# Layer 0 of a four-layer graph network: gathers of node rows held until an earlier relu has run

## The chip, the cores and the metric

The kernel runs on one core of a Trainium2 chip. The metric is the device time of one execution in microseconds (us); the number given for a kernel is the median of its runs.

## The reference, cut to what matters

A graph has 3,125 nodes with 128 features and 100,000 edges, sorted by destination. Four layers follow each other, each with a residual and a layer norm. The change is in layer 0, an attention over each node's incoming edges:

```python
hP1 = h @ P1; hP2 = h @ P2; zP3 = z @ P3             # h: nodes, z: 500 relations
pre_edge = hP1[dst] + hP2[src] + zP3[edge_type]
logit_edge = _leaky(pre_edge) @ y_w                  # 8 heads
# softmax over the edges of each destination (and the node itself) gives alpha
t_edge = hWh[src] + zWz[edge_type]
agg = segment_sum(alpha * t, dst)
out = _leaky(agg + residual_weight * h)
```

Layer 1 is a mean over neighbours with two dense layers, layers 2 and 3 are attentions with other scores. They aren't touched.

## The kernel before

**Tiles and slots.** Nodes are ordered by degree and cut into 25 tiles of 128; a node lies on a partition. Tile `t` has `CAP[t]` slots (57 down to 21): slot `s` holds the `s`-th incoming edge of each of the 128 nodes. There are 821 slots in all. `runs(t)` cuts the slots into chunks of at most `W = 8` and groups them into runs of two or three chunks; it yields 114 chunks.

**Rows.** Before the loop, a table `h_tab` of one row per node (264 floats: the part for the logits, the part for the messages, 8 more for the logits) and a table `z_tab` per relation are written to HBM. For each slot one indirect DMA (`gather`, line 102, issued by POOL) brings the row of the source node onto each of the 128 partitions of `hs`. `hs` has 8 buffers, each for one chunk.

**Two kinds of chunk.** In a "gathered" chunk (`gathered`, L842) the rows of the relation are gathered as well, into `zs` (2 buffers), and DVE adds them (L849). In a "multiplied" chunk (`multiplied`, L860), 77 of the 114, the relation's part comes by matrix products: `rb` is loaded on SP's queue (L866), DVE makes one-hots `oh` (L871), PE forms `zps` (L880), ACT copies it to `zT` (L882). In both, groups of four slots follow: PE collects the argument in `pre` (L822, L884, and L856 or L886, which read `hs`), ACT takes the relu into `low` (`logits`, L829), PE multiplies it into `lg` (L831). There are 215 such groups.

**After a run.** `masked`, `weights` and `faded` make the softmax of the run; `spread` (L915) weighs the message part of `hs` and adds it up. The `spread`s of a run are put off and issued during the next one (`owed`, `pay_some`); with the last of them a buffer of `hs` comes free. `close(t, ...)` (L941) ends a tile: `y` (L988), its layer norm `x1` (L758), which POOL writes to HBM (L991, through L105). Between chunks, `counts` (L574) makes a count matrix for layer 1, piece by piece, with one-hots on DVE and products on PE.

**Order.** Each engine runs its instructions in a fixed order. A planner sets it from the order of the program, its own costs and the dependencies; it inserts the semaphores. POOL's queue in layer 0 holds the gathers of `hs` and `zs`, a memset and a load of `x` for the next tile (`own`, L797 to L799), and the store of `x1`. A gather of `hs` may be issued once the buffer that it takes has been read for the last time.

Of the kernel before, what the change touches and what calls it, by code (L numbers as in the profile page):

```python
# [8 lines left out]
F32 = mybir.dt.float32  # L9
# [3 lines left out]
AF = mybir.ActivationFunctionType  # L13
# [7 lines left out]
NT = 25  # L21
# [30 lines left out]
CW = 512  # L52
NCW = -(-NP // CW)
AHEAD = 600


def chunks(t):
# [11 lines left out]
def runs(t):  # L69

    n = (3 * CAP[t] + 2 * W) // (4 * W)
    k, part = CAP[t] // W, CAP[t] % W
    rest = [part] * (part > 0) + [W] * (k - n)
    k = n + len(rest)
    cs, s = [], 0
    for i in range(k):
        mult = (i + 1) * n // k > i * n // k
        w = W if mult else rest.pop(0)  # L80
        cs.append((s, w, mult))
        s += w
    m = -(-k // 3)
    return [cs[i * k // m:(i + 1) * k // m] for i in range(m)]
# [3 lines left out]
def tile_gnn(ctx, tc, a, out):  # L88
    nc = tc.nc
    V, A, G, T = nc.vector, nc.scalar, nc.gpsimd, nc.tensor  # L90
# [7 lines left out]
    def indirect(ap):  # L98
        return bass.IndirectOffsetOnAxis(ap=ap, axis=0)

    def gather(dst, table, idx, **kw):
        return G.indirect_dma_start(out=dst, out_offset=None, in_=table, in_offset=indirect(idx), **kw)  # L102
# [395 lines left out]
    with tc.tile_pool(name="srcp", bufs=1) as sp, tc.tile_pool(name="srcq", bufs=2, space=PSUM) as ps:  # L498
# [28 lines left out]
        for o in range(0, NS, P):  # L527
            n = min(P, NS - o)
# [248 lines left out]
    with tc.tile_pool(name="l0", bufs=2) as wp, tc.tile_pool(name="l0s", bufs=1) as sp, \  # L777
# [5 lines left out]
        V.memset(m, LOW)  # L783
        l = sp.tile([P, NT, H], F32, name="l")
        V.memset(l, 0.0)
        nosum = sp.tile([P, D + R], F32, name="nosum")
        V.memset(nosum, 0.0)
        sums_at = sums_tab.rearrange("(t p) d -> t p d", p=P)
# [34 lines left out]
                         stop=False)  # L823
            return pre

        def logits(pre, k, lg_ps):

            low = wp.tile([P, 4, P], F32, name="low")
            A.activation(low[:, :k], pre[:, :k], AF.Relu)  # L829
            for s in range(k):  # L830
                T.matmul(lg_ps[:, s, :], low[:, s, :], yw8, start=True, stop=True)  # L831

        def halved(v, n, last=None):

            while n > 2:
                k = n // 2
                V.tensor_add(v[:, :k], v[:, :k], v[:, n - k:n])
                n -= k
            if n == 2:
                V.tensor_add(v[:, 0] if last is None else last, v[:, 0], v[:, 1])  # L840

        def gathered(hq, idx, rl, n, za, lg_ps):  # L842

            hs = wp.tile([P, W, HC], F32, name="hs", bufs=8)
            zs = wp.tile([P, W, HC + R], F32, name="zs")
            for s in range(n):
                gather(hs[:, s, :], h_tab, idx(s))
                gather(zs[:, s, :], z_tab, rl[:, s:s + 1])
            V.tensor_add(hs[:, :n], hs[:, :n], zs[:, :n, :HC])  # L849
            halved(zs[:, :, HC:], n)  # L850
            V.tensor_add(za, za, zs[:, 0, HC:])  # L851
            for s0 in range(0, n, 4):
                k = min(4, n - s0)
                pre = argument(hq, k)
                for s in range(k):
                    T.matmul(pre[:, s, :], hs[:, s0 + s, :D], ident, start=False, stop=(s == k - 1))  # L856
                logits(pre, k, lg_ps[:, s0:s0 + k])
            return hs

        def multiplied(hq, o, n, zbT, first, lg_ps):  # L860

            hs = wp.tile([P, W, HC], F32, name="hs", bufs=8)
            for s in range(n):
                gather(hs[:, s, :], h_tab, srcx[:, o + s:o + s + 1])
            rb = wp.tile([P, W * P], F16, name="rb")
            nc.sync.dma_start(rb[:, :n * P], rel_tab[o:o + n].rearrange("(o s) p -> o (s p)", o=1)  # L866
                              .to_broadcast([P, n * P]))
            ohs = []
            for i in range(NK):
                oh = wp.tile([P, W * P], BF16, name="oh", bufs=NK + 2)  # L870
                V.tensor_scalar(oh[:, :n * P], rb[:, :n * P], relid[:, i:i + 1], None, op0=OP.is_equal)  # L871
                ohs.append(oh)
            zT = wp.tile([P, W * P], F32, name="zT")
            for s0 in range(0, n, 4):
                k = min(4, n - s0)
                cols = slice(s0 * P, (s0 + k) * P)
                zps = ps1.tile([P, 4 * P], F32, name="zps")[:, :k * P]
                for i in range(NK):
                    for k2 in range(2):
                        T.matmul(zps, zq[:, i, 2 * R * k2:2 * R * (k2 + 1)], ohs[i][:, cols], start=(i + k2 == 0),  # L880
                                 stop=(i == NK - 1 and k2 == 1))
                A.activation(zT[:, cols], zps, AF.Copy)  # L882
                pre = argument(hq, k)
                T.matmul(pre[:, :k], zw[:, :D], zT[:, cols], start=False, stop=False)  # L884
                for s in range(k):
                    T.matmul(pre[:, s, :], hs[:, s0 + s, :D], ident, start=False, stop=(s == k - 1))  # L886
                logits(pre, k, lg_ps[:, s0:s0 + k])
            for s0 in range(0, n, 3):
                k = min(3, n - s0)
                t_ps = ps1.tile([P, 3, HC - D], F32, name="t_ps")  # L890
                for s in range(k):
                    T.matmul(t_ps[:, s, :], zT[:, (s0 + s) * P:(s0 + s + 1) * P], zw[:, D:], start=True, stop=True)  # L892
                V.tensor_add(hs[:, s0:s0 + k, D:], hs[:, s0:s0 + k, D:], t_ps[:, :k])  # L893
            assert n == W
            zh = wp.tile([P, W // 2, P], F32, name="zh", bufs=1)
            z3 = zT.rearrange("z (s p) -> z s p", p=P)
            V.tensor_add(zh, z3[:, :W // 2], z3[:, W // 2:])
            halved(zh, W // 2, zbT if first else None)
            if not first:
                V.tensor_add(zbT, zbT, zh[:, 0])  # L900
            return hs
# [102 lines left out]
        x1st = own(0)  # L1004
        ahead = x1st, prologue(0, x1st)
        owed = []

        def pay_some(parts):

# [3 lines left out]
        for t in range(NT):  # L1013
            n = CAP[t]
            x, (hw, hq) = ahead
            if t + 1 < NT:
                x_next = own(t + 1)
            ac, za, _ = sums_of(t)
            lg_ps = ps1.tile([P, max(CAP), H], F32, name="lg")
            zbT = wp.tile([P, P], F32, name="zbT")  # L1020
            unset = True
            for run in runs(t):
                hss = []
                for i, (s0, w, mult) in enumerate(run):
                    o = OFF[t] + s0
                    if s0 + w == n and t + 1 < NT:

                        ahead = x_next, prologue(t + 1, x_next)
                    if mult:
                        hs = multiplied(hq, o, w, zbT, unset, lg_ps[:, s0:s0 + w])  # L1030
                        unset = False
                    else:
                        hs = gathered(hq, lambda s: srcx[:, o + s:o + s + 1], rel[:, o:o + w], w, za,
                                      lg_ps[:, s0:s0 + w])
                    hss.append((s0 - run[0][0], w, hs))
                    pay_some(len(run) - i if len(runs(t)) > 1 else max(1, len(run) - 1 - i))

                    done += n_steps * w / NS
                    while done > 0:
                        next(steps, None)  # L1040
                        done -= 1

                s0, s1 = run[0][0], sum(run[-1][:2])
                with tc.high_priority(offset=AHEAD):
                    lg = masked(lg_ps[:, s0:s1], hss, s1 - s0, mask[:, OFF[t] + s0:OFF[t] + s1])
                    corr, rest = weights(wp, lg[:, :s1 - s0], s1 - s0, H, m[:, t, :], l[:, t, :])
                    faded(ac, corr, H)
                    rest()
                for q, w, hs in hss:
                    owed.append(lambda ac=ac, hs=hs, lg=lg, q=q, w=w: spread(ac, hs, lg[:, q:q + w], w))  # L1050
            owed.append(lambda t=t, x=x, hw=hw, ac=ac, za=za, zbT=zbT: close(t, x, hw, ac, za, zbT))
# [3 lines left out]
    with ExitStack() as ctx1, tc.tile_pool(name="l1", bufs=2) as wp, tc.tile_pool(name="l1s", bufs=1) as sp:  # L1055
# [11 lines left out]
        rows = sp.tile([1, 1], I32, name="rows")  # L1067
        sums = sp.tile([P, NP], F32, name="sums")
        G.memset(sums, 0.0)
        with tc.If(general > 0):  # L1070

            with tc.tile_pool(name="l1g", bufs=1) as gp, tc.tile_pool(name="l1gp", bufs=1, space=PSUM) as ps:
# [13 lines left out]
                for t in range(NT):  # L1086
# [27 lines left out]
                    for c in range(NCW):  # L1114
                        w = min(CW, NP - c * CW)
# [5 lines left out]
                for c in range(NCW):  # L1121
                    w = min(CW, NP - c * CW)
# [24 lines left out]
        for c in range(NCW):  # L1147
            w = min(CW, NP - c * CW)
# [39 lines left out]
    with tc.tile_pool(name="l2", bufs=2) as wp, tc.tile_pool(name="l2s", bufs=1) as sp, \  # L1188
# [105 lines left out]
        for t in range(NT):  # L1294
            qp = query(ps1, qb[:, t, :])
            for s0, s1, run in segments(t):
                lg = wp.tile([P, max(CAP), H2], F32, name="lg")
                parts = []
                for c0, w in run:
                    o = OFF[t] + c0  # L1300
                    parts.append(rows2(qp, pay_sb[:, o:o + w], w, lg[:, c0 - s0:c0 - s0 + w]))
                n, o = s1 - s0, OFF[t] + s0
# [8 lines left out]
            rl = wp.tile([P, H2], F32, name="rl")  # L1311
# [38 lines left out]
    with tc.tile_pool(name="l3", bufs=2) as wp, tc.tile_pool(name="l3s", bufs=1) as sp, \  # L1350
# [29 lines left out]
        for t in range(NT):  # L1380
            n = CAP[t]
# [3 lines left out]
            for s0, w in chunks(t):  # L1385
                o = OFF[t] + s0
# [12 lines left out]
            rl = wp.tile([P, 1], F32, name="rcl")  # L1399
# [4 lines left out]
            o = wp.tile([P, D], F32, name="o")  # L1404
# [22 lines left out]
```

## Time and profile before

| | |
|---|---|
| median of 3 runs | 5298.16 us (5275.42 to 5304.58) |
| the profiled execution | 5349.01 us, its span 5347.3 us |
| PE busy | 2126.7 us (40%) |
| DVE busy | 3023.3 us (57%) |
| ACT busy | 985.1 us (18%) |
| POOL busy | 2812.4 us (53%) |
| gathers of `hs` | 821, 1029 ns of POOL in the mean |
| gathers of `zs` | 205, 1019 ns in the mean |

The span runs from the first to the last instruction of the one execution that was profiled. An engine's busy time counts its own instructions; for a gather on POOL this is the instruction on POOL, and the transfer comes after it. "Idle before" is the time in which an engine stood still ahead of an instruction, with what ended it; "issue" means that the profile shows nothing that was waited for, "remote" that a semaphore ended the wait whose sender the profile could not name.

### The profile page before, as it was taken

To read this page: it belongs to the slowest core of one execution; us is meant where nothing else is said; L and a number is where in the kernel's file an instruction comes from. 1 tells how busy PE (TensorE), PEld (TensorE's weight loads), DVE (VectorE), ACT (ScalarE), POOL (GpSimd) and SP (SyncE) were. 2 spreads that over 40 slices of the span, in tenths; PEclk is the share of its full clock that TensorE was granted. 3 is DMA by queue.
4 is the path that set the end of the run, shared out by engine and by line. 5 is a ranking of instruction groups with operands and counts; after the bars stand their busy time and mean duration, and the time that the engine had idled before them with its cause. 6 is when DMAs were issued, how large, how long until landed. Compare 5 with 4: busy or idle time off the path is not lost. (4 is left out here: it accounts for less than half of the span.)

```text
span 5347.3 us, 40354 instructions
## 1 busy us (share of the span) xinstructions
PE 2126.7 (40%) x11946; PEld 1387.3 (26%) x12091; DVE 3023.3 (57%) x7369; ACT 985.1 (18%) x2562; POOL 2812.4 (53%) x2897
## 2 busy tenths in 40 slices
PE   7256767765666676776660121222323000000000
PEld 5134545544444444454330010011111000000000
DVE  8346665664555566555424566666664454454656
ACT  1023332322232333232110011111111000000000
POOL 0545545555353443444017666666662777666664
PEclk9577887777777778777885555555556555555555
DMA  2423323333222222333333333333331333223332
GB/s 84 121 72 86 95 75 91 89 92 87 79 83 77 79 82 69 89 85 86 148 137 104 102 98 114 103 105 106 121 113 61 105 98 92 86 85 92 89 88 60
DMA packets 213055, 498.40 MB, mean 93 GB/s; under 512 B 62329, under 2 KB 109100, under 8 KB 208185
## 3 DMA queue, kind: packets, MB, share of 16 engines
q0 software_dynamic: 136448, 397.65, 25.9%
q1 hardware_dynamic: 76344, 97.76, 5.7%
q8 instruction: 102, 1.67, 0.1%
q14 instruction: 161, 1.32, 0.1%
HBM read 424.65 MB, written 70.63 MB: 93 GB/s over the span
## 5 line engine op out<-in xcount | busy, mean ns | idle before, releaser
L102 POOL DMA_INDIRECT hs<-h_tab,srcx x821 | 844.9, 1029 | 839.2 <-issue 392.4
L102 POOL DMA_INDIRECT kv<-kv_tab,pay_sb x821 | 782.2, 953 | 372.2 <-issue 245.2
L102 POOL DMA_INDIRECT kv<-ktv_tab,pay_sb x821 | 803.0, 978 | 320.0 <-issue 243.7
L729 DVE TENSOR_REDUCE u<-msg 128x128 f32<-128x1024 f32 (+4 forms) x228 | 384.1, 1685 | 161.2 <-remote 100.0
L880 PE MATMUL zps<-oh,zq 128*128 128x512 bf16 x1099 | 357.7, 438 | 41.4 <-DVE bn_sd L751 10.1
L831 PE MATMUL lg<-yw,low 128*128 128x8 f32 x1642 | 234.7, 269 | 175.9 <-issue 88.6
L102 POOL DMA_INDIRECT zs<-z_tab,rel x205 | 208.8, 1019 | 172.9 <-DVE az L851 56.7
L831 PEld LDWEIGHTS lg<-yw,low 128*128 128x128 f32 x1642 | 228.6, 212 | 224.5 <-issue 107.1
L893 DVE TENSOR_TENSOR hs<-hs,t_ps 128x408 f32<-128x408 f32 (+1 forms) x231 | 122.1, 529 | 283.3 <-remote 165.8
L892 PE MATMUL t_ps<-zw,zT 128*128 128x136 f32 x1232 | 224.3, 311 | 127.5 <-DVE hs L893 78.9
L622 ACT ACTIVATE c_oha<-c_oha,srclo 128x50 bf16<-128x50 bf16 (+2 forms) x821 | 205.8, 346 | 250.1 <-DVE c_oha L570 147.0
L725 DVE TENSOR_TENSOR msg<-kv,ex 128x1024 f32<-128x1024 f32 (+4 forms) x228 | 248.8, 1103 | 3.1 <-issue 2.5
L884 PE MATMUL pre<-zT,zw 128*128 128x512 f32 x308 | 203.6, 748 | 89.0 <-ACT zT L882 44.3
L892 PEld LDWEIGHTS t_ps<-zw,zT 128*128 128x128 f32 x1232 | 193.4, 212 | 159.3 <-DVE hs L893 109.2
L740 PE MATMUL tp<-ident,an 128*128 128x128 f32 x25 | 11.5, 459 | 525.2 <-DVE qk L1206 257.0
L648 PE MATMUL c_ps<-c_ohs,c_ohd 128*128 128x128 bf16 x1300 | 128.6, 247 | 211.2 <-ACT c_sb L650 92.2
L886 PEld LDWEIGHTS pre<-ident,hs 128*128 128x128 f32 x1232 | 189.1, 221 | 74.0 <-issue 71.6
L1276 PE MATMUL xk_ps<-of,xqb 128*128 128x512 f32 x50 | 51.9, 1141 | 386.3 <-DVE xqb L758 239.6
L829 ACT ACTIVATE low<-pre 128x512 f32<-128x512 f32 (+2 forms) x215 | 123.2, 574 | 421.8 <-PE pre L886 148.0
L822 PE MATMUL pre<-identb,hq 128*128 128x512 bf16 (+3 forms) x645 | 199.3, 408 | 2.1 <-ACT hq L814 0.8
L886 PE MATMUL pre<-ident,hs 128*128 128x128 f32 x1232 | 194.5, 305 | 0.4 <-issue 0.4
L1364 DVE TENSOR_TENSOR qk<-kv,qp 128x1024 f32<-128x1024 f32 (+4 forms) x114 | 126.5, 1110 | 114.9 <-DMA kv<-ktv_tab,pay_sb 98.4
(397 smaller groups left out, 5206.3 us busy)
## 6 DMA issues: line engine op xcount, KB each, us to landing
rb<-rel_tab SPq DMA_DIRECT2D x77, 256.0 KB
c_tab<-c_sb SPq DMA_DIRECT2D x25, 768.0 KB
cs<-c_tab SPq DMA_DIRECT2D x6, 3200.0 KB
hs<-h_tab,srcx POOLq DMA_INDIRECT x821
kv<-kv_tab,pay_sb POOLq DMA_INDIRECT x821
kv<-ktv_tab,pay_sb POOLq DMA_INDIRECT x821
h_tab<-h SPq DMA_DIRECT2D x25, 132.0 KB
zs<-z_tab,rel POOLq DMA_INDIRECT x205
```

The lines of the kernel that those rows point to most:

```text
L102: return G.indirect_dma_start(out=dst, out_offset=None, in_=table, in_offset=indirect(idx), **kw)
L622: A.activation(oha[:, s // 2, 0, :, s % 2], oha[:, s // 2, 1, :, s % 2], AF.Copy, scale=srclo[:, o:o + 1])
L648: T.matmul(cps[:, j * P:(j + 1) * P], ohd[:, b // 2, :, b % 2], ohs[:, b // 2, :, b % 2], start=(i == 0), stop=(i == nb - 1))
L725: V.tensor_tensor(msg[:, :n, :].rearrange("p s (h d) -> p s h d", h=heads), val.rearrange("p s (h d) -> p s h d", h=heads), ex.unsqueeze(3 ...
L729: V.tensor_reduce(u, msg[:, :n, :].rearrange("p s d -> p d s"), AX.X, OP.add)
L822: T.matmul(pre[:, :k], hq[:, i, :], identb.unsqueeze(1).to_broadcast([P, k, P]), start=(i == 0), stop=False)
L831: T.matmul(lg_ps[:, s, :], low[:, s, :], yw8, start=True, stop=True)
L880: T.matmul(zps, zq[:, i, 2 * R * k2:2 * R * (k2 + 1)], ohs[i][:, cols], start=(i + k2 == 0), stop=(i == NK - 1 and k2 == 1))
L884: T.matmul(pre[:, :k], zw[:, :D], zT[:, cols], start=False, stop=False)
L886: T.matmul(pre[:, s, :], hs[:, s0 + s, :D], ident, start=False, stop=(s == k - 1))
L892: T.matmul(t_ps[:, s, :], zT[:, (s0 + s) * P:(s0 + s + 1) * P], zw[:, D:], start=True, stop=True)
L1364: V.tensor_mul(qk[:, :n], kv[:, :n, :D], qp.unsqueeze(1).to_broadcast([P, n, D]))
```

## The change

Each group of four slots gets a number `g`, counted through all tiles. After the relu of group `g`, ACT copies one element of `low` into `gates[g]`. Before the gathers of a chunk (in a gathered chunk: before each four of its slots), POOL copies `gates[g - 6]` into the first element of each of the rows to be gathered, on partition 0. The gathers overwrite these elements and so come after the copy; the copy comes after the relu of group `g - 6`. Six groups are three chunks of 8. The first groups, up to number 5, have no hold. A gathered chunk keeps its interleaving of `hs` and `zs` gathers in the program; the planner places them.

```diff
+LEAD = 6
...
+        gates = sp.tile([1, 2 * sum(len(run) for t in range(NT) for run in runs(t))], F32, name="gates")
...
-        def logits(pre, k, lg_ps):
+        def logits(pre, k, lg_ps, g=None):
...
             A.activation(low[:, :k], pre[:, :k], AF.Relu)
+            if g is not None:
+                A.activation(gates[:1, g:g + 1], low[:1, 0, :1], AF.Copy)
...
+        def held(rows, g):
+
+            if g is not None and g >= LEAD:
+                G.tensor_copy(rows[:1, :, 0], gates[:1, g - LEAD:g - LEAD + 1].to_broadcast([1, rows.shape[1]]))
...
-        def gathered(hq, idx, rl, n, za, lg_ps):
+        def gathered(hq, idx, rl, n, za, lg_ps, g=None):
...
             for s in range(n):
+                if s % 4 == 0:
+                    held(hs[:, s:min(s + 4, n)], None if g is None else g + s // 4)
                 gather(hs[:, s, :], h_tab, idx(s))
                 gather(zs[:, s, :], z_tab, rl[:, s:s + 1])
...
-                logits(pre, k, lg_ps[:, s0:s0 + k])
+                logits(pre, k, lg_ps[:, s0:s0 + k], None if g is None else g + s0 // 4)
...
-        def multiplied(hq, o, n, zbT, first, lg_ps):
+        def multiplied(hq, o, n, zbT, first, lg_ps, g):
...
             hs = wp.tile([P, W, HC], F32, name="hs", bufs=8)
+            held(hs, g)
             for s in range(n):
                 gather(hs[:, s, :], h_tab, srcx[:, o + s:o + s + 1])
...
-                logits(pre, k, lg_ps[:, s0:s0 + k])
+                logits(pre, k, lg_ps[:, s0:s0 + k], g + s0 // 4)
...
+        g = 0
...
+                    g += -(-w // 4)
```

In the main loop `g` goes to `multiplied` and `gathered` as an argument. The loop for nodes with more edges than slots (`behind0`) calls `gathered` without it; with this input it makes no trips.

More of the change, by code (lines that the diff above doesn't have):

```diff
@@ L1029, in tile_gnn @@
                     if mult:
-                        hs = multiplied(hq, o, w, zbT, unset, lg_ps[:, s0:s0 + w])
+                        hs = multiplied(hq, o, w, zbT, unset, lg_ps[:, s0:s0 + w], g)
                         unset = False
@@ L1033, in tile_gnn @@
                         hs = gathered(hq, lambda s: srcx[:, o + s:o + s + 1], rel[:, o:o + w], w, za,
-                                      lg_ps[:, s0:s0 + w])
+                                      lg_ps[:, s0:s0 + w], g)
+                    g += -(-w // 4)
                     hss.append((s0 - run[0][0], w, hs))
```

## The prediction

> **What bounds the kernel now.** I read the page's slices first, then the costliest groups, then busy time by stretch (the windows view), and last the timeline inside one stretch. In the page's slices each digit is the busy tenth of 1/40 of the span:
>
> ```profile
> PE   7256767765666676776660121222323000000000
> ...
> DVE  8346665664555566555424566666664454454656
> ...
> POOL 0545545555353443444017666666662777666664
> ```
>
> Layer 0 is slices 2 to 19 (208 to 2590 us by the groups of its tiles). No engine is full there: PE 1562 us of 2382 (66%), DVE 1381 (58%), POOL 1115 (47%), ACT 713 (30%). Something outside the busy time sets the pace. The groups give the gathers:
>
> ```profile
> L102 POOL DMA_INDIRECT hs<-h_tab,srcx x821 | 844.9, 1029 | 839.2 <-issue 392.4
> ...
> L102 POOL DMA_INDIRECT zs<-z_tab,rel x205 | 208.8, 1019 | 172.9 <-DVE az L851 56.7
> ```
>
> With the 0.30 us between them in the timeline (median 0.95 us each) one costs POOL 1.25 us. POOL sits idle 839 us before them: it is not short of time. Now one stretch in windows of 5 us (columns: window, length, busy PE, weight loads, DVE, ACT, POOL, granted clock, DMA share, GB/s):
>
> ```profile
> 1275.00:1280.00 5.00, 5.00 (x40) 4.38 (x39) 3.96 (x13) 1.19 (x2) 0.94 (x1) 1.00 0.11 30
> 1280.00:1285.00 5.00, 4.33 (x34) 3.11 (x35) 5.00 (x15) 3.05 (x10) 4.29 (x3) 1.00 0.19 53
> ...
> 1290.00:1295.00 5.00, 4.98 (x18) 2.61 (x18) 4.50 (x17) 3.19 (x12) 3.78 (x5) 0.51 0.56 152
> 1295.00:1300.00 5.00, 2.14 (x13) 1.10 (x12) 2.13 (x9) 0.16 (x1) 3.78 (x5) 1.00 0.44 124
> ...
> 1305.00:1310.00 5.00, 1.72 (x13) 1.32 (x11) 0.00 (x0) 0.00 (x0) 3.78 (x5) 0.50 0.41 108
> 1310.00:1315.00 5.00, 0.00 (x0) 0.00 (x0) 0.00 (x0) 0.00 (x0) 3.96 (x5) 0.50 0.40 110
> 1315.00:1320.00 5.00, 0.00 (x0) 0.00 (x0) 0.00 (x0) 0.00 (x0) 3.88 (x4) 0.50 0.36 94
> ...
> 1325.00:1330.00 5.00, 2.00 (x3) 0.96 (x4) 1.79 (x7) 1.99 (x7) 0.00 (x0) 0.50 0.00 0
> ...
> 1335.00:1340.00 5.00, 5.00 (x38) 3.79 (x38) 5.00 (x16) 2.29 (x8) 1.71 (x2) 1.00 0.25 87
> ```
>
> POOL gathers without a pause from 1280.1 to 1323.6. PE is full at first, then fades to nothing, and DVE and ACT with it (from 1290 its time is full once more, but with 18 matmuls where there were 40); all return 3 to 4 us after the last gather. The timeline shows who is late:
>
> ```profile
> 1304.43 0.59 PE L880 MATMUL zps<-oh,zq 128*128 128x512 bf16 x1
> ...
> 1322.65 0.95 POOL L102 DMA_INDIRECT hs<-h_tab,srcx  x1 [0.30 <-issue]
> ...
> 1327.36 0.60 ACT L882 ACTIVATE zT<-zps 128x512 f32<-128x512 f32 x1 [24.19 <-remote]
> ```
>
> The matmul was issued at 1304.43; its consumer is let go at 1327.33 by PE's own semaphore. So PE finished 22 us late, for no operand that is missing.
>
> I tabulated all of 310 to 2560 us like this, a **burst** being POOL work with pauses under 0.7 us. PE busy by age of the burst: 0.90 up to 5 us, 0.72 to 7.5, 0.55 to 10, 0.46 to 0.49 to 30, 0.27 beyond; after it 0.52 for 2 us, 0.68 to 4, 0.85 to 6, then 0.90 to 0.94. Against 0.92 the loss is 577 us: 32 bursts under 9 us lose 9 us (64 DMAs, 0.14 each), 27 of 9 to 13 us lose 64 (224 DMAs, 0.29 each), 34 longer ones 504 (734 DMAs, 0.69 each). **Long bursts bound layer 0**, and they are long because buffers come free several at a time: POOL leads the first use by 101 us in the median, about five chunks.
>
> **What the Trainium skill says.** "SBUF — State Buffer", section "Who interferes with whom", says PE and ACT never wait on anyone and DMA never contends with a compute engine. This trace disagrees: PE falls from 5.00 to 0.00 us of 5. I don't know the mechanism, only its shape. "Perfetto Trace Analysis", section "DMA Instruction — SWDGE (GPSIMD)", says such a row ends when descriptors are made, not when data is there; it agrees, since PE recovers only after the DMA rate has dropped to 0. "DMA: Bandwidth & Descriptors", section "Anatomy of one DMA — SWDGE (gpsimd) path", gives about 2 us fixed; the chain here has kv gathers at 2.4 us, which I use.
>
> **The change part by part.** Nothing is removed. By the order of instructions, ACT gets 215 one-element copies and POOL 133 holds; every other instruction is there once, in both. Some are placed otherwise: 255 of 4779 on POOL, 2366 of 22611 on PE, 1277 of 11826 on DVE, 262 of 3346 on ACT, 21 of 453 on SP. On PE these are swaps of a few places between the same chunk's pieces; I price them at 0, and up to 30 us either way.
>
> *Gathers held.* In the old times the relu that a chunk now waits for ended after its first gather in 102 of 110 chunks, by 42 us in the median. So nearly every hold will wait, and POOL pauses there. From that relu to the chunk's first use there were 67 us in the median; 8 gathers and a landing take 8 x 1.25 + 2.4 = 12.4. Behind a waiting hold on POOL stand z gathers of the chunk before, the x load and the x1 store. Walking the new POOL order against the old times of relus, freed buffers, y (L988) and x1 (L758), every mult chunk has its rows 10 us or more before PE uses them. The sum `hs+zs` of gathered chunks (L849 before), at its new place on DVE, has 0 to 8 us to spare in ten chunks (the second halves of their z gathers stand behind the next hold). I take 3 us late for each, **+30**; bounds 0 and 10 x 10 = 100.
>
> *Start.* Before: 83 gathers from 208 to 300, during which PE runs 6.4 us of 230 to 300. Now the first hold comes after 34 DMAs, 34 x 1.25 = 43 us, at 251; compute returns at about 254 and not 298: **-44**; bounds 0 and -60.
>
> *Steady state.* Between two holds the new POOL order has 1 to 7 DMAs (200 in all), 8 to 10 (407) or 11 to 18 (433, where z gathers join). At the losses above: 200 x 0.14 + 407 x 0.29 + 433 x 0.69 = 441 us for 577, so -136 if each hold is a pause. POOL has (1074 x 1.25 + 133 x 0.55) / 114 = 12.4 us of work per chunk, and a chunk takes about 20; it idles a third, now at the holds. But relus come in clusters some 10 us apart, where bursts join again. I take three quarters: **-100**; bounds 0 and -300 (if every DMA cost at most 0.29).
>
> *Copies.* ACT: nearest row is `corr` (L707, 128x8), 207 ns; 215 x 0.207 = 45 us beside an ACT that is 70% idle. Each waits for its relu, so the next relu starts later: **+20**, bounds 0 and 86 (0.4 each). POOL: nearest the memset of x, 259 ns, plus 0.30 to the gather: 133 x 0.55 = 73 us, hidden in POOL's idle time; if the cover is gone, +73.
>
> Sum: 30 - 44 - 100 + 20 = -94. The profiled execution took 5349.0 us (span 5347.3), 1% above the median 5298.2; it would become 5255, and the median **5205**. Layers 1 to 3 are untouched.
>
> **The rivals.**
> - *Chokes nearly gone*, 0.20: PE that stalls yields no relu, so the hold stops POOL by itself; every burst stays under 13 us. Then -300 - 44 + 20 = 4975 to 5050. Against it: gathered chunks issue up to 18 DMAs between holds.
> - *It eats itself*, 0.10: bursts join behind x1 and y waits, or the loss goes with the number of gathers; start gain against copies and waits: 5275 to 5320. That the hold doesn't bind would end here too; the 42 us speak against it.
> - *Slower: rows late*, 0.17. Now POOL leads by three chunks. A late hold delays z gathers, L849 stands at the head of DVE's queue, PE and the relu that opens the next hold wait behind it: a loop of 1 + 20 (8 rows, 8 z) + 2.4 + 2.4 (L849) + about 15 to the relu = 41 us against three chunks, 60 now. It decides once POOL waits 20 us more for y or x1, or the chunk falls below 14 us. If half the 37 gathered chunks lose 8 us, with 20 to 86 for the copies and no relief: 5370 to 5450.
>
> **How the numbers follow.** The likeliest, 0.53, gives 5205, its own range 5130 to 5270. A measurement can tell 0.5%, 26 us, from no change. Faster by more: 0.53 + 0.20 = 0.73; within: 0.10; slower: 0.17. For 8 in 10 the range takes in most of the first rival and the beginning of the last: 5020 to 5350.
>
> **What would show it.** Right: POOL's bursts of over 13 us fall from 34 to under 20; POOL's wait before the hold's copy is ended by ACT (relu or gate copy); PE's share in layer 0 rises from 66% to about 69%; the first chunks no longer show 70 dead microseconds; waits on ACT and DVE ended by "remote" shrink. Wrong: DVE waiting for L849's DMAs by over 100 us; PE waiting for `hs` at all; PE still fading in bursts of 8 as deep as in long ones; or layer 0 no shorter with its long bursts gone, which would make the fading an effect and not a cause.

## The result, and the profile after

The changed kernel took 5227.5 us (5212.6 to 5243.0), beside 5301.4 us of the kernel before on the same chip: a ratio of 0.9864, 95% interval 0.9836 to 0.9891. The prediction was 5205 us, in a range of 5020 to 5350. The profiled execution took 5243.0 us with a span of 5241.3 us. The last relu of layer 0 ends at 2466 us where it ended at 2565; what follows takes 2775 us and 2783. So the 106 us between the two spans lie in layer 0, all but 8. The medians differ by 74 us only, because the profiled execution of before was a long one.

First the page's slices of the kernel after, in the same units as before:

```profile
PE   7267676677767677777830122222232000000000
...
DVE  8346555666656666656224576556664554454646
...
POOL 0545444555545454453047666666663777666664
```

Layer 0 now ends in the 19th slice (131 us each), where it ended in the 20th (134 us each), and PE has sevens where it had sixes. Its busy time there is 1607 us of 2258 (71%). Before it was 1556 of 2357 (66%), or 68% if one fills in the 51 us of matmuls that this trace lacks (9684 records where the trace after has 9811). Then the costliest groups (busy time and mean ns of one, then the engine's idle time ahead of them with what ended it):

```profile
L103 POOL DMA_INDIRECT hs<-h_tab,srcx x821 | 848.3, 1033 | 262.0 <-issue 212.9
...
L849 POOL COPY hs<-gates 1x8 f32<-1x8 f32 (+3 forms) x133 | 41.2, 310 | 467.0 <-ACT gates L833 446.6
...
L103 POOL DMA_INDIRECT zs<-z_tab,rel x205 | 213.1, 1039 | 124.7 <-issue 55.2
```

POOL's idle time has moved. It stood 839 us ahead of the gathers of `hs`; now 262 us do, and 447 us stand ahead of the holds, ended by the copies into `gates`. Of the 133 holds, 66 waited. The start shows it in windows of 10 us (length, busy PE, weight loads, DVE, ACT, POOL, clock, DMA share, GB/s), first of before, then of after:

```profile
268.00:278.00 10.00, 0.00 (x0) 0.00 (x0) 0.00 (x0) 0.00 (x0) 7.56 (x9) 0.50 0.44 120
278.00:288.00 10.00, 0.00 (x0) 0.00 (x0) 0.00 (x0) 0.00 (x0) 7.56 (x9) 0.50 0.42 115
```

```profile
248.00:258.00 10.00, 0.00 (x0) 0.00 (x0) 0.14 (x1) 0.00 (x0) 7.71 (x10) 0.50 0.41 111
258.00:268.00 10.00, 3.88 (x12) 2.85 (x13) 2.24 (x5) 0.60 (x1) 3.62 (x4) 0.50 0.25 68
268.00:278.00 10.00, 9.22 (x71) 7.52 (x71) 7.03 (x20) 5.20 (x16) 0.46 (x2) 0.93 0.01 2
```

The first hold, at 251 us, passes without waiting (its relu ended at 217), the second stops POOL at about 263, and PE is back within 4 us. The fading inside a long burst is still there. Here is one of 24 us, in windows of 5 us, of after:

```profile
1440.00:1445.00 5.00, 4.52 (x30) 3.34 (x30) 1.78 (x4) 1.31 (x6) 4.08 (x5) 1.00 0.66 172
...
1455.00:1460.00 5.00, 2.62 (x24) 2.00 (x22) 0.52 (x1) 0.00 (x0) 3.97 (x6) 1.00 0.43 109
1460.00:1465.00 5.00, 0.00 (x0) 0.00 (x0) 0.97 (x2) 1.92 (x8) 3.78 (x5) 0.56 0.33 93
```

I made a burst table again, this time with the gathers and other DMAs of POOL alone. A burst ends at a pause of 0.7 us; bursts that begin between 310 us and the end of layer 0 are counted. "Loss" is what PE's busy time is short of 0.92 in the burst and in the first 6 us of the pause behind it.

| kernel, all with fading | bursts over 13 us | their DMAs | loss with them, us | loss per DMA | DMAs in bursts of 40 us or more |
|---|---|---|---|---|---|
| before | 34 | 727 | 474 | 0.65 | 265 |
| after | 34 | 617 | 282 | 0.46 | 109 |
| holds without a relu (`hold_free_2`) | 36 | 787 | 491 | 0.62 | 293 |
| multiplied chunks alone (`tail_free`) | 37 | 726 | 389 | 0.54 | 34 |

The traces of before and of `hold_free_2` lack 133 matmuls into `zps` (1099 records where the two others have 1232). That makes their loss too large by up to 51 us; taken off, 0.58 and 0.56 us per DMA are left. The number of long bursts is the same before and after. The longest are fewer, and a DMA in a long burst costs PE less. Times in which PE, DVE and ACT are all idle for over 2 us, after 310 us, fall from 65 with 344 us in all to 51 with 221.

### The profile page after: what moved, and what is told of

Same layout as the page of the kernel before. It is cut to its first block, busy times and chain, and to the rows that moved or that the text cites. A ratio compares the mean times of both kernels' runs of the same rounds, so it can differ in the third digit from the quotient of the medians.

```text
span 5241.3 us, 41048 instructions
## 1 busy us (share of the span) xinstructions
PE 2170.7 (41%) x12091; PEld 1405.0 (27%) x12091; DVE 3025.1 (58%) x7369; ACT 1018.4 (19%) x2777; POOL 2860.7 (55%) x3030
## 5 line engine op out<-in xcount | busy, mean ns | idle before, releaser
L892 PE MATMUL zps<-oh,zq 128*128 128x512 bf16 x1232 | 397.4, 443 | 37.1 <-DVE oh L883 20.7
L849 POOL COPY hs<-gates 1x8 f32<-1x8 f32 (+3 forms) x133 | 41.2, 310 | 467.0 <-ACT gates L833 446.6
```

## The experiments

My theory was that the wait for a relu stops POOL where PE fades (where its busy time falls off inside a burst), and that this is the gain. The rivals: any pause between the groups does it, or the new order; the start is all of it; a shorter lead alone does it; the copies on ACT do it. A condition came in that I had not foreseen. On four chips the kernel before took 4383 to 4391 us, and PE did not fade; on two others, and in the first measurement (on one of these two or a third), it took 5298 to 5363 us, and PE faded. Each ratio is to the kernel before on the same chip. So most of the experiments below ran where there was nothing to relieve, and tell only what the change costs.

| kernel | before, us | ratio (95% interval) | PE fades |
|---|---|---|---|
| the change, first measurement | 5301 | 0.9864 (0.9836 to 0.9891) | yes |
| `hold_free_2` | 5363 | 1.0026 (1.0013 to 1.0039) | yes |
| `tail_free` | 5298 | 1.0049 (1.0030 to 1.0069) | yes |
| `after_again` | 4387 | 0.9993 (0.9984 to 1.0001) | no |
| `gates_only` | 4391 | 1.0041 (1.0027 to 1.0055) | no |
| `start_only` | 4391 | 1.0033 (1.0021 to 1.0045) | no |
| `hold_free` | 4391 | 0.9975 (0.9966 to 0.9984) | no |
| `mult_only` | 4383 | 0.9988 (0.9980 to 0.9996) | no |
| `hold4` | 4386 | 1.0035 (1.0022 to 1.0048) | no |
| `lead12` | 4387 | 1.0068 (1.0055 to 1.0082) | no |
| `lead4` | 4391 | 1.0136 (1.0120 to 1.0152) | no |
| `bufs5` | 4387 | 1.0352 (1.0338 to 1.0367) | no |

**The copies alone.**

```diff
         def held(rows, g):
-            if g is not None and g >= LEAD:
-                G.tensor_copy(rows[:1, :, 0], gates[...])
+            return
```

> The 215 copies on ACT are there, the holds on POOL are not. My sum has the copies at +20 us (bounds 0 and 86): ratio to before 1.004 (1.000 to 1.016), POOL's gathers and PE's fading as before. Rival (the copies, by delaying relus or by the planner's new order on PE and DVE, make the gain themselves): 0.986 as with the whole change.

Measured: 4407.9 against 4390.8 us, +17. The copies cost what the sum had (20), 17/215 = 0.08 us each, and give nothing by themselves here. On a chip with fading they were not run alone, so there they stay a rival.

**The start alone.**

```diff
-            if g is not None and g >= LEAD:
+            if g is not None and LEAD <= g < 15:
```

> Copies as in the change, but only the holds of groups 6 to 14 (the first tile) are kept. If the start gives what the sum has (-44, or -35 as the trace after suggests: compute returns at 266 us where it was 301) against copies at 0 to 20: ratio 0.992 to 0.997. If the start is all of the gain: 0.986. If what it saves is lost again in the next bursts (12 relus later the trace after is only 13 us ahead): 0.998 to 1.003.

Measured: 2 us less than the copies alone, so nothing on this chip (what I expected was reckoned with fading): PE works through the first gathers anyway (twelve relus on from the first it is at 328 us, at 318 with the copies alone). It does not tell what the start is worth where PE fades. There the two first traces tell it: PE returns at 266 us, not at 301, but twelve relus on the lead is 13 us (369 against 382).

**Holds that wait for no relu**, on two chips:

```diff
-                G.tensor_copy(rows[:1, :, 0], gates[...])
+                G.memset(rows[:1, :, 0], 0.0)
...
-            if g is not None:
-                A.activation(gates[:1, g:g + 1], low[:1, 0, :1], AF.Copy)
```

> Each hold is there, in the same place on POOL, but as a memset of the same elements that waits for no relu; no copies on ACT. My theory (the wait for the relu is what breaks the bursts): no gain, ratio 0.997 to 1.004, long bursts as many as before (34). Rival (any instruction between the groups gives the queue a pause of half a microsecond, and that is enough, or the planner's new order is what helps): 0.986 to 0.992.

> Holds without a relu and without copies on ACT, once more, since their first run met no fading. With fading (kernel before near 5300 us): if the wait for a relu is what helps, 0.995 to 1.005 and over 600 gathers in bursts of over 13 us; if half a microsecond between the groups, or the new order of POOL's queue, is enough: 0.984 to 0.990, as with the change. Without fading: 0.996 to 0.999 as in the first run (0.9975).

Without fading it gains 0.25%, 10 us, within what I allowed; with fading it loses 0.26%, 13 us, where the changed kernel gains 1.4%, and has 787 DMAs in long bursts, as I expected of my theory. POOL's waits with fading from 310 to 2500 us (line, releaser, us in total, times, longest) show that its holds do pause POOL:

```profile
POOL hs L846 <- DVE az L926: 486.2, 36, 35.2
POOL hs L103 <- issue: 200.5, 653, 1.8
```

They pause for buffers that come free, 486 us in all. In the changed kernel the pauses are of about the same size, but ended by relus:

```profile
POOL hs L849 <- ACT gates L833: 431.8, 65, 38.6
POOL hs L103 <- issue: 198.3, 643, 1.7
```

So pauses for buffers do not help: the bursts stay as long and as costly. But this is not the changed kernel less its waits. The expectation had the holds in the same place on POOL, and in the traces they are not: with no relu to wait for, the planner put 24 of the 133 directly behind another hold (one in the changed kernel). PE, DVE and ACT run in the order of the kernel before, and so do POOL's other 1,177 instructions up to the last relu, but for 14. In the changed kernel at least 144 of these stand in another order, and 1,123 of DVE's 4,373 (counted by kind of instruction).

What the run shows is that holds on POOL in the old order, without a relu and without copies, gain nothing. **That the wait for the relu is what gains is argued, and not shown**: the planner's new order, and with fading the copies on ACT, are left as rivals. For the wait speak the 447 us that POOL stands at holds, the start, where a hold stops POOL and PE is back within 4 us, and the lower loss per DMA.

**A lead of two chunks.** `-LEAD = 6`, `+LEAD = 4`.

> Holds wait for the relu of two chunks ahead, not three. Pacing theory: more of the holds wait, bursts are shorter, PE fades less: ratio 0.975 to 0.985. Rows-late rival: rows come late, DVE waits for hs and zs at the sum of gathered chunks (line 860) for over 100 us and PE for hs, ratio 0.995 or more.

Measured: slower by 1.4%. Without fading there is nothing to relieve, and rows come late, as the rival had it (the lines are shown with the five buffers below).

**The changed kernel again, and the kernel before for a trace.** No edit.

> The changed kernel itself, unedited, once more. In the first four experiments the kernel before took 4391 us and not 5301, and PE did not fade in long bursts (0.87 busy beyond 30 us of burst, 0.27 in the trace of before). If this run meets the same conditions, there is no fading for the holds to relieve, and of my sum only the costs stay: copies +18 (measured with the gates alone) and late rows 0 to +30: ratio 1.004 to 1.012. If the gain doesn't depend on the fading: 0.986. If it meets the fading again: 0.984 to 0.989, PE fading.

> The kernel before, unedited, for a trace under the conditions of this call. Without fading: about 4390 us, PE busy over 0.8 beyond 10 us of burst, all 12091 matmul records and some 50500 records of DMA semaphores present. With fading: about 5300 us, PE below 0.5 there, and under a third of those records. A mix (5300 us with every record, or 4390 us with most of them lost) would separate the fading from the loss of records.

Measured: 0.9993 and 4379 us. The 1.4% are gone where PE does not fade. But I had expected a loss, 1.004 to 1.012: without fading too the holds save about what the copies cost. Forty relus on from the first the changed kernel is 22 us ahead (562 us against 583), at the last relu 2 us behind. Here is the kernel before on that chip, inside a burst of 346 us and 250 DMAs, in windows of 50 us:

```profile
1100.00:1150.00 50.00, 47.02 (x334) 32.42 (x331) 43.59 (x116) 24.63 (x66) 39.48 (x37) 0.93 0.50 137
...
1250.00:1300.00 50.00, 49.86 (x359) 36.17 (x358) 44.49 (x127) 24.79 (x70) 38.76 (x39) 1.00 0.44 120
1300.00:1350.00 50.00, 42.54 (x304) 29.59 (x301) 44.01 (x121) 22.09 (x63) 39.68 (x36) 0.93 0.44 123
```

POOL gathers at its full rate, as in the bursts that stopped PE on the first chip (3.8 to 4.0 us of each 5 there, 38.7 to 39.7 of each 50 here), and PE is 87% busy over the whole burst. Layer 0 takes 1709 us for 2357, PE 83% of it. Of the two mixes that would have parted the fading from the loss of records, neither came up.

**A lead of six chunks.** `-LEAD = 6`, `+LEAD = 12`.

> Holds wait for the relu of six chunks ahead, so that hardly any waits outside the start. Without fading: the copies and short pauses alone, 1.000 to 1.006, less than the changed kernel loses. With fading: between 0.990 and 1.000, since the bursts are broken only at the start; the rival that any hold helps has 0.986.

Measured: 1.0068, with 1.006, the most that I allowed, inside its interval. In the trace one hold waits for its relu, for 3.2 us. That is 12 us more than the copies alone cost. DVE stands 140 us ahead of its two operations on gathered relation rows (the sum of gathered chunks and the halving of `zs`), and 117 us with the copies alone. So later rows can account for the difference, though the two ran on two chips; why the rows are later I can't say.

**A shorter lead by buffers.** `-name="hs", bufs=8`, `+name="hs", bufs=5`, twice, in the kernel before.

> The kernel before with 5 buffers of hs for 8, no holds and no copies: the lead of the gathers is cut by buffers and not by relus. Without fading: buffers come free late, at the end of a run, so rows come late: 1.005 to 1.03. With fading: if a shorter lead is what helps, 0.986; if it is the pause at a relu, 0.997 to 1.02.

Measured: slower by 3.5%, above what I allowed. One group that waits for late rows is the sum of gathered chunks on DVE (its last part: DVE's idle time ahead of it, and what ended it). In this order: before, the change, the lead of two chunks, five buffers, all without fading:

```profile
L849 DVE TENSOR_TENSOR hs<-hs,zs 128x2112 f32<-128x2112 f32 (+7 forms) x37 | 62.1, 1677 | 51.1 <-DMA zs<-z_tab,rel 37.1 <-DMA hs<-h_tab,srcx 11.1 <-issue 2.9
```

```profile
L860 DVE TENSOR_TENSOR hs<-hs,zs 128x2112 f32<-128x2112 f32 (+7 forms) x37 | 62.1, 1679 | 83.6 <-DMA zs<-z_tab,rel 39.4 <-DMA hs<-h_tab,srcx 34.5 <-issue 9.3
```

```profile
L860 DVE TENSOR_TENSOR hs<-hs,zs 128x2112 f32<-128x2112 f32 (+7 forms) x37 | 62.1, 1679 | 107.3 <-DMA hs<-h_tab,srcx 76.9 <-DMA zs<-z_tab,rel 17.3 <-DMA x_tab<-x,node_d 12.6
```

```profile
L849 DVE TENSOR_TENSOR hs<-hs,zs 128x2112 f32<-128x2112 f32 (+7 forms) x37 | 62.1, 1679 | 192.9 <-DMA hs<-h_tab,srcx 133.8 <-DMA zs<-z_tab,rel 45.1 <-issue 14.0
```

At this sum it is 51, 84, 107 and 193 us. But DVE also halves `zs` (adds its slots up pairwise), at times ahead of the sum, and waits there for the same rows. The halving before, and then with the change:

```profile
L837 DVE TENSOR_TENSOR zs<-zs 128x128 f32<-128x128 f32 (+3 forms) x54 | 17.2, 319 | 41.5 <-DMA zs<-z_tab,rel 34.1 <-issue 7.2
L840 DVE TENSOR_TENSOR zs<-zs 128x64 f32<-128x64 f32 x33 | 7.3, 221 | 26.8 <-DMA zs<-z_tab,rel 26.7
```

```profile
L841 DVE TENSOR_TENSOR zs<-zs 128x128 f32<-128x128 f32 (+3 forms) x54 | 17.2, 321 | 20.8 <-DMA zs<-z_tab,rel 20.7
L844 DVE TENSOR_TENSOR zs<-zs 128x64 f32<-128x64 f32 x33 | 7.2, 218 | 10.5 <-DMA zs<-z_tab,rel 10.4
```

Sum and halving together wait 119, 115, 163 and 246 us. So the change itself moves the wait from one operation to the other and does not make rows later without fading; a lead of two chunks and five buffers do, in the order of the ratios (0.9993, 1.0136, 1.0352). A short lead as such gains nothing without fading. With fading it was not tried, so there a shorter lead, by whatever means, stays a rival.

**Holds ahead of multiplied chunks alone**, and a copy only where a hold reads it:

```diff
-                if s % 4 == 0:
-                    held(hs[:, s:min(s + 4, n)], None if g is None else g + s // 4)
...
-            if g is not None:
+            if g in used:
                 A.activation(gates[:1, g:g + 1], low[:1, 0, :1], AF.Copy)
```

> The change with holds only ahead of multiplied chunks, and a copy on ACT only for the groups that such a hold reads (72 or so for 215). Without fading: the copies cost +18 x 72/215 = +6; DVE's idle time ahead of the sum of gathered chunks returns from 84 us to the 51 to 55 us of the kernel before, and what the pacing gained in the first tiles (about 30 us) stays: ratio 0.988 to 0.996. If it is not the holds of gathered chunks that make rows late: 0.997 to 1.001, with the idle time at 80 us. With fading: 0.980 to 0.990, since z rows no longer sit behind a hold but bursts of up to 24 gathers are left.

Measured: 0.9988, and 82 us idle at L860: not the 0.988 to 0.996 of my theory, but what I had named for the other case. The holds of gathered chunks are not what moves the wait to that sum. With the halving of `zs` it is 114 us, 119 in the kernel before, so rows are no later in all. Up to relu 204 this kernel is 25 us ahead of the kernel before (1830 against 1855 us), and it loses nearly all of that in one stall. DVE's and POOL's waits from 1780 to 1915 us:

```profile
DVE hs L860 <- DMA hs<-h_tab,srcx: 23.7, 1, 23.7
```

```profile
POOL x_tab L106 <- DVE x L759: 24.4, 1, 24.4
POOL hs L851 <- ACT gates L835: 14.1, 2, 10.1
```

POOL's queue waits 24.4 us for the layer norm that it is to store, and the rows of the next gathered chunk stand behind that store; the kernel before waits there too (26.4 us at the longest), but has those rows already.

**The same without holds in the last four tiles.**

```diff
-            if g is not None and g >= LEAD:
+            if g is not None and LEAD <= g < 186:
```

> As the version with holds ahead of multiplied chunks only, and without holds from group 187 on (the last four tiles). There the trace of that version loses 24 us at once: POOL waits 24.4 us for the layer norm of the tile before (line 759) to store it, the rows of the next gathered chunk stand behind the store, and DVE waits 23.7 us for them at line 860; with a lead of five chunks the same store costs nothing. If that is what eats the gain of the first tiles: that stall is gone, and the ratio without fading is 0.990 to 0.996. If the tail is bound otherwise (all kernels end layer 0 at 1910 to 1915 us): 0.998 to 1.000. With fading: 0.980 to 0.990.

It met a chip with fading, so the question of the tail stays untried. The ratio is 1.0049, outside the 0.980 to 0.990 that I expected. With fading, then, waits for relus ahead of multiplied chunks alone gain nothing, though POOL stands 272 us at them (310 to 2530 us, 46 waits). Nor is it enough that the longest bursts are gone: 34 DMAs are left in bursts of 40 us or more. A gathered chunk puts up to 16 more DMAs between two such holds (36 at the most in this trace), and over 13 us long there are as many DMAs as before (726), at 0.54 us each. The four free tiles at the end may have a part in it.

**Holds ahead of each four slots everywhere.**

```diff
-            held(hs, g)
             for s in range(n):
+                if s % 4 == 0:
+                    held(hs[:, s:min(s + 4, n)], g + s // 4)
```

> The change with a hold ahead of each four slots in multiplied chunks too, each on its own group's relu (the second four wait for g + 1 - 6). With fading: if it is the number of gathers between two relu waits that counts, PE fades less and the ratio is below the change's 0.986: 0.970 to 0.983; if the clusters of relus join the short groups to the same bursts, 0.983 to 0.990; if waiting later makes rows late (DVE's idle time at line 860, 3 to 21 us in the runs with fading, over 60), 0.992 or more. Without fading: 0.998 to 1.006.

It met no fading: 1.0035, 16 us slower in all, about 18 behind the changed kernel by the ratios. With fading it was not tried, so no version here beats both kernels on both kinds of chip; `hold_free` is best without fading (0.9975), the change with it.

## Why the prediction was right, and where not

The range, 5020 to 5350 us, takes in the 5298 us of the kernel before, so that the time fell into it says little. That it came near 5205 is in part luck: of two terms that were to gain, one was not kept, and on four of the chips met later the gain of the whole would have had no cause to appear.

- **Long bursts bound layer 0.** It fits the chip of the measurement: with holds ahead of all chunks PE loses less in bursts and the time falls (0.9864); with holds that leave the bursts it does not (1.0026). It is no property of the kernel alone: on four chips of six or seven the same bursts do not stop PE, and on the one of these where the change ran again it was worth nothing.
- **Steady state, -100.** I had it as 136 less a quarter. PE's loss in all bursts, counted as in the table, fell from 542 to 366 us (up to 51 of this being the records that the trace of before lacks), yet layer 0 got only 98 us shorter in these two executions. Part came back outside the bursts: 10 us and more after a burst PE is 0.77 busy where it was 0.94. From the medians: -74, less late rows of 14 and copies of 17, leaves -105 for start and steady state together, for -144 predicted. The prediction's own loss of 577 us is a little large: its windows view has PE busy 1527 us of the 2250 from 310 to 2560 us, 543 short of 0.92.
- **"Bursts of over 13 us fall from 34 to under 20": wrong.** By the prediction's own count they are 36. I had taken each hold for a pause; half of the holds pass at once. What changed is which bursts are cut. A relu that comes late while PE stands still stops POOL, one that comes in time lets it go on, so more of those that remain long should be those in which PE keeps pace. This reading fits the lower loss per DMA (0.58 to 0.46 us, the lacking matmuls taken off), but it is argued: no run shows a single burst with and without its hold, and `tail_free` has fewer DMAs in the longest bursts still and gains nothing.
- **Start, -44.** The first hold was to stop POOL at 251 us; it passed, since its relu had run at 217, and the second stopped it. PE returned 35 us earlier, of which 13 were left twelve relus on: a second burst, from 278 to 334 us with 42 DMAs, held PE at 0.54. Sixty relus on, the changed kernel was 20 us behind (908 us against 887). So in these two executions all of the 98 us was won after that, in the steady state, and the start was worth nothing in the end.
- **Late rows, +30.** The sum of gathered chunks does wait with fading, 2.2 us before and 21.4 after, but mostly for rows of `hs` (14.1) and less for the `z` rows that I had named (5.3). The halving of `zs` waited 14.7 us before and 10.0 after, so together it is +14, half of the term. Without fading it is about -5 (119 to 115).

```profile
L849 DVE TENSOR_TENSOR hs<-hs,zs 128x2112 f32<-128x2112 f32 (+7 forms) x37 | 62.1, 1677 | 2.2 <-DMA zs<-z_tab,rel 1.9 <-issue 0.2
```

```profile
L860 DVE TENSOR_TENSOR hs<-hs,zs 128x2112 f32<-128x2112 f32 (+7 forms) x37 | 62.0, 1677 | 21.4 <-DMA hs<-h_tab,srcx 14.1 <-DMA zs<-z_tab,rel 5.3 <-issue 1.8
```

- **Copies, +20.** +17 by the run of them alone, without fading. POOL's holds cost little, as supposed: without relus they are 10 us faster without fading (`hold_free`) and 13 slower with it (`hold_free_2`).
- **The other signs.** POOL's wait ahead of the hold is ended by ACT; PE waits for rows of `hs`, which I had as a sign of being wrong, but for 1.5 us in all of layer 0; waits ended by "remote" fell (the copy of `c_sb` on ACT, 186 to 92 us). "DVE over 100 us at the sum" stayed away.
- **The rivals.** Without fading the change lands in the "within 0.5%" that I gave 0.10, though by another way than the one named. The slower rival, rows late, is what the lead of two chunks and the five buffers show. Its sum was off: half of 37 chunks at 8 us is 148 us, with 20 to 86 for the copies 5466 to 5532 us, and not 5370 to 5450.

## What to carry to other kernels

Before a stall is put down to the order of a kernel, compare the same kernel on a second chip: here the wait that bound layer 0 showed on some chips only, and so did the gain. A wait that ties a producer to the progress of its consumer went with a gain where bare pauses did not. To show that it is the wait, take it out and keep everything else: where a planner sets the order, look at the order too, since taking out the relu here brought the old order back. What such a wait costs is lead: look for what else stands in that queue, here a store that waits for a layer norm, since the lead was paying for it. And add up every operation that waits for the same rows before calling them late.

## What the runs showed of the hardware

The chips fall in two kinds, a fifth apart: 5298 to 5363 us for the kernel before, or 4383 to 4391. Each was met at one time only, so whether it is the chip or its condition then, no run tells. Nor is it layer 0 alone: what follows takes 2783 us in `before` and 2464 in `before_again`. A gather costs POOL about the same on both: 0.95 us in the median and 0.30 to the next (1.03 us in the mean with fading, 1.08 without). The traces differ in another way too: those with fading hold 13,697 to 14,567 records of semaphore increments by DMAs, those without 50,478 to 50,527, from nearly the same instructions. So where PE stalls, the recording loses most of these events, in all four traces of the one kind and none of the ten of the other. Whether a jam on the way of such events stalls the engines, or the recording itself does, or both follow from a third thing, no run here tells.

The late instruction fetch that one might suspect does not show. Blocks of 16 KB on one of the queues, which I take for PE's instructions from their number (102, for 24,182 matmuls and weight loads), arrive ahead of PE. The Trainium skill, "Runtime: NRT & Kernel Launch", section "Instruction fetch mechanics", has 256 instructions to such a block and says that an engine fetches the next one while it executes the current one. Counted so, an estimate, each block of layer 0 arrives 535 to 683 instructions ahead of PE with fading (`before`) and 503 to 563 without (`before_again`), so the trace agrees.

"SBUF — State Buffer", section "Who interferes with whom", which the prediction found at odds with the first trace, agrees with the chips without fading: there PE is 87% busy through 250 DMAs without a pause. The section speaks of conflicts at the ports of SBUF; that PE stalls in the first trace does not show such a conflict.
